# Seven products instead of eight for the last three query projections of an attention kernel, with their operand sums kept in spare parts of other tiles

## The chip, the cores and the metric

The kernel runs on one core of one Trainium2 chip. Its time is the device time of one execution in microseconds (us), given as the median of several runs.

The engines go by these names: TensorE (PE in the profile; PEld is its weight load), VectorE (DVE), ScalarE (ACT), GpSimd (POOL) and SyncE (SP, which issues most of the DMAs here). Each works through its own queue in order and waits on semaphores for the others.

## The reference

Everything is fp32: one sequence of 1,024 rows, 512 wide. Causal attention has 32 query heads on 8 key and value heads, 128 wide. It sits between two layer norms and a residual, and a feed-forward layer with a routed low-rank part follows. Cut to what matters:

```python
n = layernorm(x)                                   # (1024, 512)
q = (n @ w_q).reshape(S, 8, 4, 128)                # 8 groups of 4 query heads
k = (n @ w_k).reshape(S, 8, 128)
v = (n @ w_v).reshape(S, 8, 128)
scores = einsum("qhgd,khd->hgqk", q, k) * 128 ** -0.5
probs = softmax(where(causal, scores, -inf))
attn = einsum("hgqk,khd->qhgd", probs, v).reshape(S, 4096) @ w_o
x = x + layernorm(attn)
h = layernorm(x)
y = h @ base_W.T + base_b + lora(h, softmax router over 15 logits)
out = x + layernorm(y)
```

## The kernel before, in words

**Blocks and pairs.** A block is one key/value group g (0 to 7, with its four query heads) and one tile t of 128 query rows: 64 blocks, `blocks[i]`, in the order in which they run. Two neighbouring blocks, tiles 2u and 2u + 1 of one group, make a pair; `pairs[m]` holds blocks 2m and 2m + 1. The first 24 pairs go through groups 0 to 5. The last eight (from block N2 = 48 on) take the groups 6 and 7 in turn, with u in the order 0, 3, 2, 1. So the last blocks are:

| pair m | blocks i | group, tiles | key columns up to |
|---|---|---|---|
| 26, 27 | 52-53, 54-55 | 6 and 7, tiles 6 and 7 | 1024 |
| 28, 29 | 56-57, 58-59 | 6 and 7, tiles 4 and 5 | 768 |
| 30, 31 | 60-61, 62-63 | 6 and 7, tiles 2 and 3 | 512 |

**A block.** The loop over i computes a block's scores in four parts (`scores(g, t, j)`, four times 32 rows for four heads). Each part is one or two matmuls into PSUM, then on VectorE the mask (L622) and the row maximum (L624), on ScalarE the exponential (L629) and, after a reciprocal (L636), the scaling (L637), and on VectorE a transpose into the tile T (L643). The scaling and the transpose of a part are issued inside the next part's call, those of the last part inside the next block's first. GpSimd writes zeros to the end of the row (`memset`, L627). After the fourth part 16 DMAs on SyncE's queue copy T, rearranged, into the tile K (`to_keys`). T and K are "block-row tiles": one of each for even tiles t and one for odd ones (`turn_tile`), of 3,584 and 4,096 words per partition, of which a block fills (t + 1) x 512.

**What fills TensorE between the parts.** Between the score parts stand pieces of other work, cut into four shares by their number of columns (`run_share`):
- `pv`: the value products (`po`) of the block two before, one piece of 512 columns for each key tile;
- `o`: the output projection (`pO`) of block i - 3 where that belongs to group 7, after which a row is complete and its norm steps follow; `o_pair` is the same for a pair of the other groups;
- `begins` and `ends`: the router and the feed-forward layer of a finished row;
- `q`: the query projection of the next pair, in the odd blocks. It must be done when the next block's first scores start.

Steps of the norms and of the router on VectorE and GpSimd are put in a list (`defer`) and taken from it one or more at each score part (`work_off`).

**Two forms of the query projection.** `project_q` multiplies directly: 16 matmuls of 256 columns, two PSUM banks, two ScalarE copies (L429). `project_q_halves` splits weights and tokens into two by two quarters and forms the product from seven products of sums instead of eight products of quarters: 28 matmuls of 128 columns, four PSUM banks taken from a pool of three, one ScalarE copy (L480), and six VectorE additions (`add`, L454) that merge the products into the query tile qT. It needs sums of the weight quarters (`combine_w`, L145, four GpSimd operations for each load of a group's weights) and of the token quarters (`combine_x`, L188, four more for each u). Pairs in `QW`, which are 2 to 27, use this form; pairs 0, 1 and 28 to 31 use the direct one.

**What sets the order.** `keep` and `order` pin an instruction behind everything already written for its engine; VectorE's additions at L454 and ScalarE's copies of queries are not pinned. The tile framework adds the waits. The tiles `wq` have one buffer: the next group's weights (`load_q`, SyncE, at the start of an even block) wait for the last product that reads the old ones.

Of the kernel before, what the change touches and what calls it, by code (L numbers as in the profile page):

```python
# [9 lines left out]
F32 = mybir.dt.float32  # L10
I32 = mybir.dt.int32
AF = mybir.ActivationFunctionType
ALU = mybir.AluOpType
AX = mybir.AxisListType

P = 128
# [6 lines left out]
def kernel(  # L23
# [33 lines left out]
    nc = tc.nc  # L57
# [4 lines left out]
    NT = S // P  # L62
    KC = H // P
    QB = 512
    NQB = S // QB
    TPB = QB // P
    PQ = 2 * P
    SQ = P // R
    NSUB = P // SQ
# [11 lines left out]
    turn = ctx.enter_context(tc.tile_pool(name="turn", bufs=1))  # L81
# [6 lines left out]
    pairs = [(g, u) for g in range(G - 2) for u in range(NT // 2)]  # L88
    pairs += [(g, u) for u in (0, 3, 2, 1) for g in (G - 2, G - 1)]
    blocks = [(g, 2 * u + e) for g, u in pairs for e in range(2)]  # L90
    N = len(blocks)
    N2 = (G - 2) * NT
    QW = range(2, N2 // 2 + 4)

    def keep(ins):
        return tc.keep_in_program_order(ins)
# [5 lines left out]
    def matmul(*args, **kw):  # L102
        keep(nc.tensor.matmul(*args, **kw))  # L103
# [6 lines left out]

    def turn_tile(kind, g, t):

        size = (NT - 1 + t % 2) * NSUB * P
        return turn.tile([P, size], F32, tag=f"{kind}{t % 2}", name=f"{kind}_{g}_{t}")

    weights = {}

# [119 lines left out]
    xnT = [big.tile([P, KC, QB], F32, tag=f"xnT{b}", name=f"xnT_{b}") for b in range(NQB)]  # L237
# [72 lines left out]
    def bank(name):  # L310
        return ps_m.tile([P, 512], F32, tag="pm", name=name)
# [104 lines left out]
    def project_q(g, u):  # L416

        pm = {}

        def get(j):  # L420
            if j % 2 == 0:
                pm[0] = bank(f"pq_{g}_{u}_{j}")
            return pm[0][:, ts(j % 2, PQ)]

        def finish(j):
            if j == 0:
                qTs[g, u] = act.tile([P, PQ // SQ, R, SQ], F32, tag="qT", name=f"qT_{g}_{u}")
            if j % 2:
                nc.scalar.copy(  # L429
                    qTs[g, u][:, :, j - 1 : j + 1, :].rearrange("p s h q -> p h s q"),  # L430
                    pm[0].rearrange("p (h s q) -> p h s q", h=2, q=SQ),
                )

        def term(j, c):
            w = weights["q", j // 2]
            assert w[0] == g
            rhs = xnT[u * PQ // QB][:, c, ts(u % (QB // PQ), PQ)]
            return w[1][:, c, ts(j % 2, D)], rhs

        work = []  # L440
        for j in range(R):
            terms = [lambda j=j, c=c: term(j, c) for c in range(KC)]
            if j == 0:
                ends = lambda pm: finish(0)
            else:
                ends = lambda pm, j=j: finish(j)
            work += chained(lambda j=j: get(j), terms, ends, PQ)
        return work
# [4 lines left out]
    def add(dst, src, to):  # L453
        nc.vector.tensor_tensor(dst, src, to, ALU.add)  # L454

    def project_q_halves(m):


        g, u = pairs[m]
        hk = KC // 2  # L460
        pm = {}

        def half(e, h):

            return both(e)[:, h]

        def both(e):
            q = qTs[g, u][:, ts(e, NSUB), :, :]
            return q.rearrange("p s (x h) q -> p x s (h q)", x=2)

        def each(x):

            return qTs[g, u].rearrange("p s (x h) q -> p x s (h q)", x=2)[:, x]

        def merge(b):

            one, two = pm[b][:, 0], pm[b][:, 1]
            if b == 0:
                q = each(0).rearrange("p (e s) n -> p e s n", e=2)
                nc.scalar.copy(q, one.unsqueeze(1).to_broadcast([P, 2, NSUB, 2 * SQ]))  # L480
                add(half(0, 0), two, half(0, 0))
            elif b == 1:
                add(half(1, 0), one, half(1, 0))
                add(half(1, 1), two, half(1, 0))
            elif b == 2:
                add(half(0, 1), one, half(1, 1))
                add(half(1, 0), two, half(1, 0))
            else:
                add(both(1), one.unsqueeze(1).to_broadcast([P, 2, NSUB, 2 * SQ]), both(1))

        def piece(n, c, k):
            i, b, x = PRODUCTS[n], n // 2, n % 2
            if n == c == k == 0:
                qTs[g, u] = act.tile([P, PQ // SQ, R, SQ], F32, tag="qT", name=f"qT_{g}_{u}")
            if x == c == k == 0:
                whole = bank(f"pq_{g}_{u}_{b}")
                pm[b] = whole.rearrange("p (x s n) -> p x s n", x=2, s=NSUB)
            assert weights["sq"] == (g,) and weights["tx of"] == u
            matmul(
                pm[b][:, x, :, ts(c, SQ)],  # L500
                weights["sq", 0][i][:, k, ts(c, D)],
                weights["tx"][i][:, k, :].rearrange("p (s q) -> p s q", q=SQ),
                start=(k == 0),
                stop=(k == hk - 1),
            )
            if c == 1 and k == hk - 1 and (x == 1 or n == 6):
                merge(b)

        return [
            (P, lambda n=n, c=c, k=k: piece(n, c, k))  # L510
            for n in range(7)
            for c in range(2)
            for k in range(hk)
        ]
# [50 lines left out]
        return project_halves(f"v{gv}", u, ("sv", gv), lambda w, x: (x, w), quarters)  # L565

    turned, keyed = {}, {}

    def turn_view(w, t):
        n = t + 1  # L570
        return w[:, : n * NSUB * P].rearrange("p (b s k q) -> p b s k q", b=R, s=NSUB, k=n)
# [29 lines left out]
    def rescale_scores():  # L601
        if "rescale" in score_tile:
            score_tile.pop("rescale")()
# [325 lines left out]
    c, d, e, f = (blocks[k][1] for k in (N - 6, N - 5, N - 2, N - 1))  # L929
    later = {}  # L930

    def projections(i):
# [10 lines left out]
        elif i % 2 and m < len(pairs) and i not in (N2 + 1, N2 + 5):  # L943
            q = project_q_halves(m) if m in QW else project_q(*pairs[m])
        first = GV
# [114 lines left out]
    def attend(i):  # L1060
        return weighted_values(*blocks[i])

    ready = []
    for i in range(N):
        loads(i)
        q, other = projections(i)
        pv = attend(i - 2) if i >= 2 else []
        o, o_pair, ends, begins = [], [], [], []
        for t in complete(i, 3):
            o = project_o(*blocks[i - 3])  # L1070
        if i % 2 == 0 and i >= 4 and blocks[i - 4][0] < G - 1:
            if i == 4:
                rescale_scores()
            o_pair = project_o_pair(*pairs[i // 2 - 2])
        for t in complete(i, 6, 7):
            ends = sum(ffn_out(t), [])
        for t in complete(i, 5):
            begins = ffn_router(t)

        rest = o + weave(o_pair, other + pv[:2] + begins[1:] + pv[2:])  # L1080
        if i in (N2, N2 + NT // 2):
            rest = weave(o_pair, pv) + other
        if i == N2 + 1:
            rest = pv[:3] + other + pv[3:]

        if i % 2 and i // 2 + 1 in QW and blocks[i][1] > 1 and i > 3:
            cut = len(rest) * 3 // 5
            q, rest = weave(q, rest[:cut]), rest[cut:]
        then = begins[:1] + q + ends[:-1] + rest[:4] + ends[-1:] + rest[4:]
        shares = [n / NSUB for n in range(NSUB + 1)]  # L1090
        if o_pair and blocks[i][0] % 2 == 0 and blocks[i][1] == 2 and i < N2:

            shares[3] = 0.8
        for n in range(NSUB):
            scores(*blocks[i], n)
            run_share(then, shares[n], shares[n + 1])
            m = i // 2 + 1
            if i % 2 == 0 and m in QW:
                if n == 0 and i < N2:
                    combine_x(pairs[m][1], m)  # L1100
                if n == (1 if i < N2 else 0):
                    combine_q(m)
            g, t = blocks[i]
            if g % 2 and g + 1 < G and n == 1:
                if t == 6:
                    combine_k(g + 1)
                if t == 7:
                    combine_v((g + 1) // GV)
            if (i, n) in ((N2, 3), (N2 + 1, 2), (N2 + 2, 2)):
                combine_x(i - N2 + 1, 0)  # L1110
        if i == 1:
            combine_o(0)
        if i == NT:
            prepare_ffn()
        if i == NT + 4:
            prepare_map()
        for t in complete(i, 2):
            reload_x(t)
        ready += complete(i, 7, 8)
        for t in [t for t in ready if ("done", t) in state]:  # L1120
            ready.remove(t)
            ffn_store(t)

        if i >= NT and blocks[i - 2][1] == 0 and blocks[i - 2][0] < G - 1:
            combine_o(blocks[i - 2][0])
# [79 lines left out]
```

## Time and profile before

| what | value |
|---|---|
| median of 3 runs | 1059.7 us (1059.08 to 1059.84) |
| the profiled execution, its own time | 1059.33 us |
| its span, first to last instruction | 1057.3 us |
| TensorE busy | 1043.3 us, 99% |
| VectorE busy | 748.2 us, 71% |
| ScalarE busy | 477.9 us, 45% |
| GpSimd busy | 267.5 us, 25% |
| mean granted TensorE clock | 0.998 |

The last blocks begin, by TensorE's timeline, at 869.30 (block 56), 891.46 (57), 913.50 (58), 929.96 (59), 948.27 (60), 966.69 (61), 985.30 (62) and 997.97 us (63). What follows 1006 us is the end of the last rows' feed-forward layer.

How to read the lines: in the timeline a line begins with the start in us from the span's beginning and the busy time of the merged instructions; then engine, source line, operation, output <- inputs by the program's names, their shapes, and xN, the number of records. An fp32 matmul is two records. A bracket gives the idle time of the engine just before, and what ended it. In the answer on waits a line is: who waited, for whom, us in total, times, and the longest.

### The profile page before, as it was taken

How to read it: one execution, taken by the hardware profiler on the slowest of the kernel's cores; microseconds unless marked ns; L12 is line 12 of the kernel's file. 1: busy time of each engine (PE TensorE's matmuls, PEld its weight loads, DVE VectorE, ACT ScalarE, POOL GpSimd, SP SyncE). 2: the span in 40 equal slices, each digit the busy share in tenths (PEclk: the TensorE clock that was granted, in tenths of full speed). 3: DMA queues.
4: the chain of work that ended last, by engine and by line, in shares of the span. 5: the costliest groups of instructions: out<-in, count | busy, mean ns of one | idle time of the engine just before them, and what ended most of it. 6: DMA issues, size and time to landing. Idle time of an engine off the chain costs nothing.

```text
span 1057.3 us, 15637 instructions
## 1 busy us (share of the span) xinstructions
PE 1043.3 (99%) x4864; PEld 732.0 (69%) x4864; DVE 748.2 (71%) x1831; ACT 477.9 (45%) x962; POOL 267.5 (25%) x502
## 2 busy tenths in 40 slices
PE   8999999999999999999999999999999999999996
PEld 7766677767787676767787667767888466566453
DVE  4576657876687766887487866886667966576666
ACT  2655435553244544554244544654234654454421
POOL 2613125241131214241130312442162110111212
PEclk9999999999999999999999999999999999999999
DMA  5145352563125452453324452464333674543331
GB/s 189 32 125 138 77 122 70 146 152 87 33 54 160 95 118 63 120 150 82 73 51 122 108 113 66 131 168 112 87 108 87 166 173 104 140 106 99 81 91 40
DMA packets 78513, 111.99 MB, mean 106 GB/s; under 512 B 18176, under 2 KB 49920, under 8 KB 78432
## 3 DMA queue, kind: packets, MB, share of 16 engines
q1 hardware_dynamic: 74960, 105.71, 39.8%
q0 software_dynamic: 2096, 3.46, 1.4%
q10 hardware_dynamic: 1376, 1.84, 0.5%
q8 instruction: 39, 0.64, 0.3%
q14 instruction: 42, 0.34, 0.1%
HBM read 33.34 MB, written 2.10 MB: 34 GB/s over the span
## 4 chain that ended last, share of the span: by engine, by line
PE 92%; DVE 3%; SPq 2%; ACT 1%; DMA 1%; issue 1%; POOL 0%; POOLq 0%; ACTq 0%; DVEq 0%
PE po L103 22%; PE s L103 21%; PE pq L103 19%; PE pv L103 5%; PE pe L103 4%; PE pk L103 4%; PE pa L103 4%; PE pf L103 3%; PE pO L103 3%; PE pc L103 2%; PE pb L103 2%; PE pd L103 2%; SPq L109 2%; PE pl L103 1%; DVE nmax L624 1%
## 5 line engine op out<-in xcount | busy, mean ns | idle before, releaser
L637 ACT ACTIVATE p<-p,rec 128x32 f32<-128x32 f32 (+31 forms) x256 | 188.1, 735 | 233.7 <-DVE rec L636 177.1
L103 PE MATMUL po<-K,v 128*128 128x512 f32 x576 | 280.5, 594 | 0.7 <-DMA wo<-in_w_o_dram 0.6
L103 PE MATMUL s<-kT,qT 128*128 128x512 f32 (+15 forms) x768 | 272.4, 464 | 0.8 <-ACT p L629 0.7
L629 ACT ACTIVATE p<-s,nmax 128x32 f32<-128x32 f32 (+31 forms) x256 | 179.3, 700 | 165.5 <-DVE nmax L624 151.0
L643 DVE STREAM_TRANSPOSE T<-p 128x128 f32<-128x128 f32 (+7 forms) x256 | 197.6, 774 | 54.2 <-ACT p L637 42.8
L103 PEld LDWEIGHTS s<-kT,qT 128*128 128x128 f32 x768 | 140.5, 190 | 117.0 <-issue 105.2
L624 DVE TENSOR_REDUCE nmax<-s 128x1 f32<-128x32 f32 (+31 forms) x256 | 180.1, 703 | 7.2
L103 PEld LDWEIGHTS po<-K,v 128*128 128x128 f32 x576 | 103.5, 190 | 59.9 <-issue 50.6
L627 POOL MEMSET p<- 128x96 f32 (+2 forms) x192 | 29.1, 156 | 420.3 <-DVE T L643 387.0
L622 DVE TENSOR_TENSOR s<-s,smask 128x32 f32<-128x32 f32 x256 | 47.8, 187 | 86.4 <-PE s L103 85.6
L103 PE MATMUL pq<-xnT,wq 128*128 128x128 f32 (+1 forms) x608 | 97.5, 308 | 0.0
L454 DVE TENSOR_TENSOR qT<-pq,qT 128x256 f32<-128x256 f32 x156 | 70.0, 460 | 35.9 <-ACT qT L480 19.6
L103 PEld LDWEIGHTS pq<-xnT,wq 128*128 128x128 f32 x608 | 87.5, 191 | 11.3 <-issue 6.6
L188 POOL TENSOR_TENSOR tx<-xnT 128x256 f32<-128x256 f32 x52 | 37.8, 727 | 183.4 <-PE pv L103 95.3
L674 ACT COPY attnT<-po 128x512 f32<-128x512 f32 x64 | 37.3, 583 | 74.0 <-PE po L103 73.7
L103 PE MATMUL pa<-wo,attnT 128*128 128x256 f32 x224 | 58.5, 385 | 0.0
L103 PEld LDWEIGHTS pq<-tx,wq 128*128 128x128 f32 x416 | 53.0, 192 | 7.9 <-issue 7.5
L103 PE MATMUL pq<-tx,sq 128*128 128x128 f32 x416 | 57.5, 275 | 0.0
L103 PEld LDWEIGHTS pq<-tx,sq 128*128 128x128 f32 x416 | 53.4, 192 | 5.7 <-issue 5.0
L103 PE MATMUL pq<-tx,wq 128*128 128x128 f32 x416 | 55.4, 275 | 0.0
L103 PEld LDWEIGHTS pa<-wo,attnT 128*128 128x128 f32 x224 | 41.1, 190 | 14.1 <-issue 9.3
L636 DVE RECIPROCAL rec<-total 128x1 f32<-128x1 f32 x256 | 39.2, 153 | 15.7 <-ACT p L629 14.5
(152 smaller groups left out, 1286.2 us busy)
## 6 DMA issues: line engine op xcount, KB each, us to landing
K<-T SPq DMA_DIRECT2D x128, 128.0 KB, 2.4
K<-T SPq DMA_DIRECT2D x128, 112.0 KB, 2.3
wq<-in_w_q_dram SPq DMA_DIRECT2D x27, 512.0 KB, 5.0
K<-T SPq DMA_DIRECT2D x128, 96.0 KB, 2.2
K<-T SPq DMA_DIRECT2D x128, 80.0 KB, 2.1
wo<-in_w_o_dram SPq DMA_DIRECT2D x32, 256.0 KB, 3.9
K<-T SPq DMA_DIRECT2D x108, 64.0 KB, 2.0
K<-T SPq DMA_DIRECT2D x113, 48.0 KB, 2.0
```

The costliest lines, as they stand in the source:

```text
L103: keep(nc.tensor.matmul(*args, **kw))
L109: keep(by.dma_start(dst, src))
L188: nc.gpsimd.tensor_tensor(dst, p, q, ALU.subtract)
L454: nc.vector.tensor_tensor(dst, src, to, ALU.add)
L622: keep(nc.vector.tensor_tensor(s[:, n - SQ : n], s[:, n - SQ : n], smask, ALU.add))
L624: keep(nc.vector.tensor_reduce(nmax, s[:, :n], AX.X, ALU.max, negate=True))
L627: nc.gpsimd.memset(p[:, n:full], 0.0)
L629: keep(nc.scalar.activation(p[:, :n], s[:, :n], AF.Exp, bias=nmax, accum_out=total))
L636: keep(nc.vector.reciprocal(rec, total))
L637: keep(nc.scalar.mul(p[:, :n], p[:, :n], rec))
L643: nc.vector.transpose(turned[g, t][:, :, j, :, :].rearrange("p b k q -> p k b q"), p[:, :full].rearrange("p (k b q) -> p k b q", b=R, q=SQ),)
L674: copy = nc.scalar.copy(o, po)
```

## The change

Pairs 29, 30 and 31 (the new list `QL`) go over to the seven-product form. Pair 28 stays direct.

Their sums get no tiles of their own. Blocks 54 and 55 (group 7, tiles 6 and 7) are the last that fill T and K to the end. From them on `turn_tile` returns the same four tiles again (`long_tiles`) instead of new ones. The following blocks fill at most six of their eight parts (five of seven in the even ones), and `spare` gives out the parts behind: three for the weight sums s1, s2, s4 (two in the even T, one in the odd T) and two for the four token sums t1 to t4 (in the even K). The fourth weight sum replaces the quarter a21 in place, as before.

The sums are written as a list (`last_sums`) when part 2 of the even block before is issued, and pinned on GpSimd in portions (`LATE`): two after part 2 and two after part 3 of the even block, the remaining four (the token sums, for pairs 29 and 30) after part 0 of the odd block. Pair 31 uses the token sums of pair 30.

In the odd blocks 57, 59 and 61 the query pieces move: they stood at the head of the block's pieces and now stand before the last four (`rest[cut:]`), and what stood behind them (pO, the value products, the router's products) comes earlier.

```diff
-    QW = range(2, N2 // 2 + 4)
+    QL = range(N2 // 2 + 5, N // 2)
+    QW = [*range(2, N2 // 2 + 4), *QL]
...
     def turn_tile(kind, g, t):
 
+        if (kind, t % 2) in long_tiles:
+            return long_tiles[kind, t % 2]
         size = (NT - 1 + t % 2) * NSUB * P
-        return turn.tile([P, size], F32, tag=f"{kind}{t % 2}", name=f"{kind}_{g}_{t}")
+        w = turn.tile([P, size], F32, tag=f"{kind}{t % 2}", name=f"{kind}_{g}_{t}")
+        if (g, t) in blocks[N2 + 6 : N2 + 8]:
+            long_tiles[kind, t % 2] = w
+        return w
+
+    def spare(kind, e, n):
+
+        at = (NT - 3 + e + n) * NSUB * P
+        return long_tiles[kind, e][:, at : at + NSUB * P].rearrange("p (k n) -> p k n", k=KC // 2)
+
+    def last_sums(m):
+
+        g, u = pairs[m]
+        w = [weights["q", i][1] for i in range(2)]
+        hk = KC // 2
+        a11, a12, a21, a22 = w[0][:, :hk], w[0][:, hk:], w[1][:, :hk], w[1][:, hk:]
+        s1, s2, s4 = spare("T", 0, 0), spare("T", 0, 1), spare("T", 1, 0)
+        xp = xnT[u * PQ // QB][:, :, ts(u % (QB // PQ), PQ)]
+        b11, b12, b21, b22 = xp[:, :hk, :P], xp[:, :hk, P:], xp[:, hk:, :P], xp[:, hk:, P:]
+        t1, t2, t3, t4 = (spare("K", 0, n // 2)[:, :, ts(n % 2, P)] for n in range(4))
+        todo = [
+            (s1, a21, a22, ALU.add),
+            (s2, s1, a11, ALU.subtract),
+            (a21, a11, a21, ALU.subtract),
+            (s4, a12, s2, ALU.subtract),
+        ]
+        if weights["tx of"] != u or m == QL[0]:
+            todo += [
+                (t1, b12, b11, ALU.subtract),
+                (t2, b22, t1, ALU.subtract),
+                (t3, b22, b12, ALU.subtract),
+                (t4, b21, t2, ALU.subtract),
+            ]
+        weights["sq", 0] = (a11, a12, s4, a22, s1, s2, a21)
+        weights["sq"] = (g,)
+        weights["tx"] = (b11, b21, b22, t4, t1, t2, t3)
+        weights["tx of"] = u
+        return todo
+
+    long_tiles = {}
+
+    LATE = {(e, n): k for e, ks in enumerate(((0, 0, 2, 2), (4, 0, 0, 0))) for n, k in enumerate(ks)}
...
-        if i % 2 and i // 2 + 1 in QW and blocks[i][1] > 1 and i > 3:
+        if i % 2 and i // 2 + 1 in QW and blocks[i][1] > 1 and 3 < i < N2:
             cut = len(rest) * 3 // 5
             q, rest = weave(q, rest[:cut]), rest[cut:]
         then = begins[:1] + q + ends[:-1] + rest[:4] + ends[-1:] + rest[4:]
+        if i % 2 and i // 2 + 1 in QL:
+            cut = max(4, len(rest) - 4)
+            then = begins[:1] + ends[:-1] + rest[:4] + ends[-1:] + rest[4:cut] + q + rest[cut:]
...
             scores(*blocks[i], n)
             run_share(then, shares[n], shares[n + 1])
             m = i // 2 + 1
-            if i % 2 == 0 and m in QW:
+            if i % 2 == 0 and m in QL and n == 2:
+                todo.extend(last_sums(m))
+            if i >= N2 + NT and i // 2 + 1 in QL:
+                for dst, p, q, op in [todo.pop(0) for _ in range(min(LATE[i % 2, n], len(todo)))]:
+                    keep(nc.gpsimd.tensor_tensor(dst, p, q, op))
+            if i % 2 == 0 and m in QW and m not in QL:
```

The bound `3 < i < N2` leaves the weaving of earlier blocks as it was. At block 53, where the old condition held too, there are no query pieces and no router or feed-forward pieces, so that the order there is the same.

More of the change, by code (lines that the diff above doesn't have):

```diff
@@ L492, in piece @@
             i, b, x = PRODUCTS[n], n // 2, n % 2
+            assert not todo
             if n == c == k == 0:
@@ L567 @@
     turned, keyed = {}, {}
+    todo = []
     def turn_view(w, t):
```

## The prediction

> **What bounds the kernel now.** I read the page's totals and its chain first, then TensorE's waits, then its timeline where the edited work stands, then VectorE's timeline at the same places.
>
> ```profile
> span 1057.3 us, 15637 instructions
> ...
> PE 1043.3 (99%) x4864; PEld 732.0 (69%) x4864; DVE 748.2 (71%) x1831; ACT 477.9 (45%) x962; POOL 267.5 (25%) x502
> ...
> PE 92%; DVE 3%; SPq 2%; ACT 1%; DMA 1%; issue 1%; POOL 0%; POOLq 0%; ACTq 0%; DVEq 0%
> ```
>
> TensorE (PE) is busy 99% of the span and is 92% of the chain that ended last. VectorE has 29% of the span idle and GpSimd 75%. All that TensorE waited for, in the whole span, is this:
>
> ```profile
> PE idle L106 <- POOL ident masks.py:199: 1.5, 1, 1.5
> ...
> PE s L103 <- ACT p L629: 0.7, 2, 0.3
> PE pc L103 <- DVE acc L748: 0.7, 1, 0.7
> PE po L103 <- DMA wo<-in_w_o_dram: 0.6, 1, 0.6
> ...
> PE pd L103 <- DVE hw L836: 0.3, 1, 0.3
> ```
>
> No wait in this answer, small ones included, is as long as 2 us. So TensorE's instruction stream is the time, and two things count: how long the stream becomes, and whether a new wait appears in it. Its length has to be read as pitch, start to start, because the durations overlap. These are seven-product queries of pair 26, the form that the last three pairs get, and then the ordinary queries of pair 30, one of the three:
>
> ```profile
> 815.88 1.67 PE L103 MATMUL s<-kT,qT 128*128 128x512 f32 x4
> 817.39 1.72 PE L103 MATMUL pq<-tx,wq 128*128 128x128 f32 x14
> 818.95 1.06 PE L103 MATMUL pq<-xnT,sq 128*128 128x128 f32 x8
> 819.84 1.06 PE L103 MATMUL pq<-tx,sq 128*128 128x128 f32 x8
> 820.73 1.72 PE L103 MATMUL s<-kT,qT 128*128 128x512 f32 x4
> ```
>
> ```profile
> 931.53 3.19 PE L103 MATMUL pq<-xnT,wq 128*128 128x256 f32 x14
> 934.55 1.35 PE L103 MATMUL s<-kT,qT 128*128 128x512 f32 x4
> 935.73 3.19 PE L103 MATMUL pq<-xnT,wq 128*128 128x256 f32 x14
> 938.76 1.40 PE L103 MATMUL s<-kT,qT 128*128 128x512 f32 x4
> 939.99 1.03 PE L103 MATMUL pq<-xnT,wq 128*128 128x256 f32 x4
> ```
>
> Each fp32 matmul is two records. From 817.39 to 820.73 there are 30 records of 128 columns: 3.34/30 = 0.111 us each. From 931.53 to 934.55 there are 14 of 256 columns: 0.216 us each; 935.73 to 938.76 gives the same. A 512-column matmul (two records) takes 0.858 us in the same timeline.
>
> **The change, part by part.** *TensorE, removed and added.* An ordinary pair is 16 matmuls, 32 records x 0.2162 = 6.92 us. A seven-product pair is 28 matmuls, 56 records x 0.1113 = 6.23 us. Three pairs: 3 x 0.69 = **2.05 us saved**. This is 0.19% of the run, so even the whole of it stays just inside the 0.2% that a measurement of this kernel can tell from no change.
>
> [...]
>
> *ScalarE and VectorE.* A pair loses one of its two 0.585 us ScalarE copies and gains five adds of 128x256 (0.42 us) and one of 128x512 (0.69): 2.8 us of VectorE. In the windows of the three blocks that compute queries (57, 59, 61) VectorE is busy 11.3 of 22.0, 12.2 of 18.3 and 9.8 of 18.6 us. It fits; only the time of the last add matters (below).
>
> *GpSimd.* Three weight groups of four 128x512 sums (1.27 us each in the trace) and two token groups of four 128x256 (0.73): 15.2 + 5.8 = 21 us on an engine that is a quarter busy. The orders that count: the sums of group 29 run after scores 2 and 3 of block 56 and the token sums after scores 0 of block 57 (897 to 900 behind the waiting `acc` addition of 895.85), and the first product that needs them starts at 903.7. In block 59 the token sums stand behind `rstd_h` (934.2) and end at about 937.4, t2 at 936.0; product 3 needs it at 937.4 and product 4 needs t3 at 938.3. Queued behind these sums are pad memsets and the next `rstd` powers; both have microseconds until a transpose or a norm needs them. Cost on the path 0; if the cover went, each 0.73 us sum late would stop TensorE for as long.
>
> *SyncE.* No DMA is added. The next load of `wq` waits for the last product that reads the old one (the twentieth of 28 pieces): 906.3 in block 57, 941.3 in block 59, while SyncE reaches that load at 907.43 and 944.28. So the copies of T to K queued behind it are not held.
>
> *What moves.* In blocks 57, 59 and 61 the products go from the front to just before the last pieces of PV. I laid the pieces on the pitches, a block's four quarters being cut by columns; times are those of the shortened stream:
> - Block 57: four pO and one po, scores, three po and 6 products, scores, 19 products, scores, 3 products (end 909.4), four po (3.43 us); block 58's scores at 912.85 (913.50 now).
> - Block 59: turn, two po, router products, one po, scores, 12 products, scores, 14, scores, 2 (end 944.36), three po (2.57 us); block 60's scores at 946.93.
> - Block 61: 17 products before the last scores, 1 after (end 979.8), four po; block 62's scores at 983.25.
>
> PV of block 57's K now starts at 930.9 instead of 940.9; the last of the 16 copies of that K is issued at 926.1 and lands 2.1 us later, at 928.2. pO in block 57 starts at 892.6; its `attnT` copy is done at 892.25. Block 59's router products start at 932.6, hT's copy ends by 931.7. All three fit, the second by only 0.3 us. The products take four PSUM banks in turn from a pool of three, where ordinary queries took two: in block 59 the third (940.4) reuses the router's `pl`, free when `hw` is made at about 939.9; a late route there would stop TensorE by its lateness.
>
> *The new wait.* The last add (128x512) writes half of the whole query tile, so the next block's first scores wait for it. It stands on VectorE behind the last scores' work of the block. For seven-product queries and for block 59 the trace has these rows:
>
> ```profile
> 818.83 1.10 DVE L643 STREAM_TRANSPOSE T<-p 128x896 f32<-128x896 f32 x1
> 819.85 2.50 DVE L454 TENSOR_TENSOR qT<-pq,qT 128x256 f32<-128x256 f32 x5
> ```
>
> ```profile
> 945.28 0.96 DVE L624 TENSOR_REDUCE nmax<-s 128x1 f32<-128x768 f32 x1
> 946.15 0.97 DVE L643 STREAM_TRANSPOSE T<-p 128x768 f32<-128x768 f32 x1
> ```
>
> The first pair shows that adds queue behind the row maximum and the transpose: products ended at 820.73, the adds at 822.35. With block 59's new order: last scores end at 943.91, mask and maximum (0.96) to 945.3, transpose (0.97) to 946.2, then the row's next deferred step, which is y's statistics (0.65 + 0.18 + 0.15) because the router moved ahead, to 947.2, then the add to 947.9, some 948.0 with the hand-over, against 946.93 when TensorE gets there: up to 1.1 us of waiting. The add is not pinned and can slip in front of the statistics: then 947.0, a wait of 0.1. By the same sum block 57's add ends at 912.8 against 912.85, and block 61's at 983.0 against 983.25. Bounds: 0 (all adds early, or the four free `rest` pieces cover them) and, if five adds come as one run of 2.50 us behind the statistics, 1.8 + 2.9 + 1.5 = 6.2 us. I take 0.8 us: block 59's sum mostly in force, the other two met.
>
> Sum: -2.05 + 0.8 = **-1.25 us**. Made on the profiled execution: span 1057.3 to about 1056.05, with the 2.03 us around it (its own time is 1059.33) 1058.1. That execution is 0.37 us under the median of the runs, 1059.7, so the median becomes **1058.5**.
>
> **The rivals.** *The adds come late in all three pairs (slower).* One mechanism: VectorE runs its queue in order, and the five adds of a pair bunch as they did at 819.85, after the last scores' maximum, transpose and statistics. Place: first scores of blocks 58, 60, 62. Price: 6.2 us in full, net +4.15, 1063.9. It decides as soon as the three waits add up to more than 2.05 us, and is beyond 0.2% above 4.2 us. For it: the run of five at 819.85. Against: in the new order 24 or more of the 28 products lie before the last scores, so four of the adds can run in VectorE's idle stretch before them (2.90 us of idle before the scores of 909.41). More likely in part than in full.
>
> *No wait at all.* All adds slip in and block 61's earlier pO takes its norm steps out of blocks 62 and 63, where VectorE is busy 9.3 of 12.7 and 7.0 of 8.0 us; the tail's single wait of 0.29 us could go too. -2.05 to -2.4: 1057.3 to 1057.65. Against: block 59's margin is negative by my sum.
>
> *The sums are not free of the tile they lie in.* If waits were kept per tile, not per part, the token sums of block 57 would wait for the copies of K of block 56 (last landing about 908, needed at 903.7) and those of block 59 for block 58's (about 946, needed at 937): 5 + 11 us of stall, net about +14, 1074. The trace speaks against it, on a tile of the same kind, the input rows held in a K tile:
>
> ```profile
> 4.54 0.69 DVE L331 BATCH_NORM_STATS2 stats_x<-K_x 128x6 f32<-128x512 f32 x1 [4.54 <-DMA K_x<-in_x_dram]
> ...
> 13.57 0.69 DVE L331 BATCH_NORM_STATS2 stats_x<-K_x 128x6 f32<-128x512 f32 x1 [1.38 <-DMA K_x<-in_x_dram]
> ```
>
> Row 0 is read at 4.54 while another row of the same tile makes VectorE wait for its DMA until 13.57: parts are waited for separately.
>
> **How the numbers follow.** My forecast, waits of 0.1 to 1.6 us in sum, 1057.7 to 1059.2: 0.62. No wait or a small gain more: 0.14, of which about 0.10 lie beyond 0.2% below (under 1057.6). Late adds: 0.18, split between within 0.2% (0.09) and beyond (0.09). Tile-wide waits, or sums late on GpSimd: 0.06, all slower. Faster 0.10, same 0.71, slower 0.19. The range takes the forecast, the no-wait case and the late adds up to waits of 3.5 us: 1057.3 to 1061.2.
>
> **What would show it.** Right: `pq` records of 256 columns in blocks 57, 59 and 61 replaced by 56 of 128 at 0.111 us; scores of block 58 beginning about 0.65 us earlier than 913.50; a single TensorE wait on VectorE's `qT` of 0.3 to 1.1 us at about 947; GpSimd 21 us busier; no wait on GpSimd or on a DMA of K. Wrong: waits on `qT` at all three block starts (late adds), TensorE waiting for the sums on GpSimd or GpSimd waiting for SyncE's copies (tile), a pitch well over 0.111 us with the sums as weights.

## The result, and the profile after

The changed kernel takes **1057.63 us** in the median of 12 runs (1056.39 to 1058.32), against 1059.61 us for 12 runs of the kernel before: ratio 0.9978, 95% interval 0.9971 to 0.9985. In a second set of runs it was 1057.57 against 1059.89 us, ratio 0.9979 (0.9970 to 0.9988). So it is faster by about 2 us, 0.2%, which is nearly all that the shorter stream offers; 1058.5 was predicted.

The page of the changed kernel: its span, the busy line and the chain by engine.

```profile
span 1056.3 us, 15824 instructions
...
PE 1041.1 (99%) x4936; PEld 732.1 (69%) x4936; DVE 757.2 (72%) x1849; ACT 477.0 (45%) x959; POOL 288.0 (27%) x522
...
PE 92%; DVE 3%; SPq 2%; ACT 1%; DMA 1%; issue 1%; POOL 0%; POOLq 0%; DVEq 0%; ACTq 0%
```

TensorE is still 99% busy and 92% of the chain. GpSimd has 20.5 us more than before (288.0 against 267.5) and VectorE 9.0 more; neither shows in the chain. Three lines of the answer on TensorE's waits (who waited, for whom: us in total, times, longest):

```profile
PE ptx_x L109 <- DVE K_x L390: 1.2, 1, 1.2
PE s L106 <- DVE qT L500: 0.9, 1, 0.9
...
PE po L106 <- DMA K<-T: 0.2, 1, 0.2
```

The only wait for a query tile, 0.9 us, lies at 57.45 us, at the first scores of block 4, where both kernels issue the same instructions. It is not one of the three that the prediction spoke of, but it shows what such scores wait for. VectorE there in the changed kernel, then TensorE:

```profile
56.92 0.72 DVE L500 TENSOR_TENSOR qT<-pq,qT 128x256 f32<-128x256 f32 x2
...
59.74 0.67 DVE L500 TENSOR_TENSOR qT<-pq,qT 128x512 f32<-128x512 f32 x1
```

```profile
57.45 1.24 PE L106 MATMUL s<-kT,qT 128*128 128x512 f32 x4 [0.85 <-DVE qT L500]
```

The two additions at 56.92 belong to the third of the four PSUM banks. The first of them writes the half of the query tile that the even block reads and ends at 57.31 (0.39 us); the scores start 0.14 us later, and 2.3 us before the last addition (128x512, at 59.74) begins. The kernel before has the same place, VectorE and then TensorE:

```profile
56.15 0.72 DVE L454 TENSOR_TENSOR qT<-pq,qT 128x256 f32<-128x256 f32 x2
...
58.98 0.68 DVE L454 TENSOR_TENSOR qT<-pq,qT 128x512 f32<-128x512 f32 x1
```

```profile
56.68 1.24 PE L103 MATMUL s<-kT,qT 128*128 128x512 f32 x4
```

In both profiles block 4's first scores start 0.53 us after the third bank's additions begin (56.15 and 56.68, 56.92 and 57.45), whether TensorE's line shows idle time before them (0.85 us) or none, and 2.3 us before the last addition begins. So the profile before already held the answer to the question on which the prediction turned: do the even block's scores wait for the last addition?

The wait for `K<-T` (0.2 us) is new and small; the experiment e8 below takes it up.

The span fell by only 1.0 us (1057.3 to 1056.3), less than the medians, and that can be placed. Block 57 begins at 892.49 here and began at 891.46 before, though TensorE's order of instructions is identical up to there. Some 0.7 us of this arises at block 4: the value products before its first scores start at 54.66 and 54.71, the scores at 56.68 and 57.45. In the nine profiles of the changed kernel and its variants block 57's start lies anywhere from 891.05 to 892.49. From block 57 on the comparison is sharp. The length of each block is the difference between the starts of its own and the next block's first `s` records in TensorE's timeline:

| profile | 57 | 58 | 59 | 60 | 61 | 62 | 63 to the end | 57 to the end |
|---|---|---|---|---|---|---|---|---|
| before | 22.04 | 16.46 | 18.31 | 18.42 | 18.61 | 12.67 | 59.33 | 165.84 |
| after | 21.39 | 16.46 | 17.66 | 18.41 | 17.95 | 12.68 | 59.26 | 163.81 |
| e0_changed | 21.39 | 16.46 | 17.66 | 18.42 | 17.95 | 12.67 | 59.28 | 163.83 |
| e1_order_only | 22.05 | 16.46 | 18.31 | 18.42 | 18.60 | 12.68 | 59.27 | 165.79 |
| e2_products_first | 31.04 | 16.46 | 21.94 | 18.43 | 17.94 | 12.68 | 59.16 | 177.65 |
| e3_gate_even_half | 21.40 | 16.45 | 18.63 | 18.50 | 17.95 | 12.67 | 59.25 | 164.85 |
| e4_products_last | 21.39 | 16.54 | 18.85 | 18.49 | 17.95 | 12.67 | 59.61 | 165.50 |
| e5_sums_once | 21.39 | 16.45 | 17.67 | 18.41 | 17.95 | 12.67 | 59.31 | 163.85 |
| e7_two_pairs | 22.05 | 16.45 | 17.66 | 18.42 | 17.95 | 12.67 | 59.24 | 164.44 |
| e8_split_copies | 21.39 | 16.45 | 17.67 | 18.42 | 17.95 | 12.67 | 59.34 | 163.89 |

Blocks 57, 59 and 61, which compute the queries, are 0.65, 0.65 and 0.66 us shorter; no other block changed by more than 0.01. The sum is 1.96 us, and 2.03 to the end. Between two profiles an unchanged block agrees to 0.02 us, so that these rows tell much more than the medians, whose runs spread over 1 to 2 us.

The place that should have held the wait, in the changed kernel. First TensorE's timeline of block 59 up to block 60's first scores:

```profile
936.64 1.95 PE L106 MATMUL pq<-xnT,wq 128*128 128x128 f32 x16
938.43 1.06 PE L106 MATMUL pq<-K,T 128*128 128x128 f32 x8
939.32 1.40 PE L106 MATMUL s<-kT,qT 128*128 128x512 f32 x4
940.56 1.95 PE L106 MATMUL pq<-K,wq 128*128 128x128 f32 x16
942.34 1.06 PE L106 MATMUL pq<-xnT,T 128*128 128x128 f32 x8
943.24 0.61 PE L106 MATMUL pq<-K,T 128*128 128x128 f32 x4
943.68 1.46 PE L106 MATMUL s<-kT,qT 128*128 128x512 f32 x4
944.98 0.61 PE L106 MATMUL pq<-K,T 128*128 128x128 f32 x4
945.42 2.74 PE L106 MATMUL po<-K,v 128*128 128x512 f32 x6
948.00 0.65 PE L106 MATMUL s<-kT,qT 128*128 128x288 f32 x2
```

The 56 `pq` records lie where the prediction laid them: 12 matmuls, scores, 14, scores, 2. The sources K and T are the spare parts with the sums. From 936.64 to 939.32 there are 24 records at 0.112 us. Then three value products (six `po` records) and, at 948.00 with no idle time, block 60's first scores. VectorE at the same time:

```profile
943.40 1.73 DVE L500 TENSOR_TENSOR qT<-pq,qT 128x256 f32<-128x256 f32 x4
...
946.29 0.97 DVE L691 STREAM_TRANSPOSE T<-p 128x768 f32<-128x768 f32 x1
947.18 0.65 DVE L334 BATCH_NORM_STATS2 stats_y<-y 128x6 f32<-128x512 f32 x1
947.75 0.67 DVE L500 TENSOR_TENSOR qT<-pq,qT 128x512 f32<-128x512 f32 x1
948.34 0.17 DVE L336 BATCH_NORM_AGGREGATE mv_y<-stats_y 128x2 f32<-128x6 f32 x1
```

The last addition (128x512) starts at 947.75, behind the transpose and half of y's statistics, and VectorE's next instruction starts at 948.34; by its own duration the addition ends at 948.42. Counted from block 59's start (930.34 here, 929.28 in the prediction's schedule) the addition ends after 18.0 us, where I had summed 18.6, and the scores begin after 17.66 us, where I had 17.65. So the addition is indeed late, by 0.34 us at least. But the scores began before it had ended: they did not wait for it. At blocks 58 and 62 the last addition ends before TensorE gets there (913.22 against 913.88, 981.82 against 984.36), so these two places say nothing about the wait.

### The profile page after: what moved, and what is told of

It reads as the page before. It is cut to its first block, busy times and chain, and to the rows that moved or that the text cites. A ratio compares the mean times of both kernels' runs of the same rounds, so it can differ in the third digit from the quotient of the medians.

```text
span 1056.3 us, 15824 instructions
## 1 busy us (share of the span) xinstructions
PE 1041.1 (99%) x4936; PEld 732.1 (69%) x4936; DVE 757.2 (72%) x1849; ACT 477.0 (45%) x959; POOL 288.0 (27%) x522
## 4 chain that ended last, share of the span: by engine, by line
PE 92%; DVE 3%; SPq 2%; ACT 1%; DMA 1%; issue 1%; POOL 0%; POOLq 0%; DVEq 0%; ACTq 0%
PE po L106 22%; PE s L106 21%; PE pq L106 18%; PE pv L106 5%; PE pe L106 4%; PE pk L106 4%; PE pa L106 4%; PE pf L106 3%; PE pO L106 3%; PE pc L106 2%; PE pb L106 2%; PE pd L106 2%; SPq L112 2%; PE pl L106 1%; DVE nmax L672 1%
## 5 line engine op out<-in xcount | busy, mean ns | idle before, releaser
L685 ACT ACTIVATE p<-p,rec 128x32 f32<-128x32 f32 (+31 forms) x256 | 188.1, 735 | 240.9 <-DVE rec L684 184.0
L500 DVE TENSOR_TENSOR qT<-pq,qT 128x256 f32<-128x256 f32 x174 | 77.9, 461 | 38.2 <-ACT qT L526 21.1
L106 PEld LDWEIGHTS pq<-xnT,wq 128*128 128x128 f32 x560 | 75.4, 191 | 9.5 <-issue 6.6
L106 PE MATMUL pq<-xnT,wq 128*128 128x128 f32 (+1 forms) x560 | 81.6, 293 | 0.0
```

What stands on the lines that cost most here:

```text
L685: keep(nc.scalar.mul(p[:, :n], p[:, :n], rec))
```

## The experiments

The competing theories. **A**: the last addition writes only the half of the query tile that the pair's odd block reads; the even block, which comes next, needs only the additions before it, and the shorter stream comes through whole. **B**: the prediction, in which the last addition is waited for. **C**: the gain comes from the moved order, not from the products. Every run has its block lengths in the table above; they tell the theories apart better than the medians do.

**e0_changed**: the changed kernel beside the others, with no edit.

> The changed kernel itself, beside the others on one chip. Theory A (the last addition writes only the odd half of the query tile, so that the next block's first scores do not wait for it, and the shorter stream comes through whole): 2.0 us under the kernel before. Theory B (the prediction: the last addition is waited for, about 0.8 us of the 2.05 is lost): 1.2 us under it. Theory C (the gain comes from the moved order, not from the products): also 2.0 us under it.

1057.57 us, ratio 0.9979 (0.9970 to 0.9988), 2.3 us under the kernel before, and the same block lengths as in the first profile. Against B's 1.2 us; A and C stand.

**e1_order_only**:

```diff
-            q = project_q_halves(m) if m in QW else project_q(*pairs[m])
+            q = project_q_halves(m) if m in QW and m not in QL else project_q(*pairs[m])
...
-            if i % 2 == 0 and m in QL and n == 2:
+            if False and m in QL and n == 2:
```

> The queries of pairs 29 to 31 in the direct form (32 records of 256 columns), but at the late place of the change; no sums on GpSimd. Theory A: the stream is as long as before, 1059.6, within 0.4 us. Theory C: about 2 us under the kernel before, as the change. Theory B says the same as A here, since the two ScalarE copies of the direct form take 0.6 us and 2.6 to 3.4 us of value products stand behind them.

1059.34 us against 1059.89, ratio 0.9997 (0.9988 to 1.0005); blocks 57, 59 and 61 are 22.05, 18.31 and 18.60 us, as before the change. The moved order by itself gains nothing, C falls.

**e7_two_pairs**:

```diff
-    QL = range(N2 // 2 + 5, N // 2)
+    QL = range(N2 // 2 + 6, N // 2)
```

> Only pairs 30 and 31 in the seven-product form and at the late place; pair 29 direct and at the head, as before. Theory A: two thirds of the gain, 1.35 us under the kernel before, in the trace 0.65 to 0.69 us less in blocks 59 and 61 and nothing in block 57. Theory C or a fixed gain at one place: 0 or 2.0 us under it.

1058.41 us against 1059.54, ratio 0.9989 (0.9980 to 0.9998). The table shows the dose: block 57 back at 22.05, blocks 59 and 61 at 17.66 and 17.95. Each pair brings its own 0.65 us.

**e3_gate_even_half**: the wait that the prediction supposed, made real by a multiplication by 1.0 behind the last addition, on the half that it does not write.

```diff
                 add(both(1), one.unsqueeze(1).to_broadcast([P, 2, NSUB, 2 * SQ]), both(1))
+                if m in QL:
+                    keep(nc.vector.tensor_scalar(both(0), both(0), 1.0, None, ALU.mult))
```

> The change plus, for pairs 29 to 31, a VectorE multiplication of the even half of the query tile by 1.0 (about 0.55 us) pinned behind the last addition: now the next block's first scores do wait for work behind the last addition, the wait that the prediction supposed. Theory A: block 60's first scores wait about 0.9 us (the addition ends at 948.3 in the changed kernel's trace, plus 0.55 and the hand-over, against TensorE at 948.0), block 58's 0 to 0.1, block 62's none; 0.9 us over the changed kernel. Theory B (the scores wait for the last addition already): 0.5 us or less over the changed kernel, and the trace of the changed kernel should have shown a wait of its own.

1058.89 us against 1059.89 before, ratio 0.9991 (0.9982 to 1.0000), 1.3 us over e0_changed by the medians and 1.0 by the blocks. TensorE in this run:

```profile
945.39 2.74 PE L106 MATMUL po<-K,v 128*128 128x512 f32 x6
948.93 0.72 PE L106 MATMUL s<-kT,qT 128*128 128x288 f32 x2 [0.81 <-DVE ve_y L338]
```

and VectorE:

```profile
947.72 0.67 DVE L500 TENSOR_TENSOR qT<-pq,qT 128x512 f32<-128x512 f32 x1
948.31 0.17 DVE L336 BATCH_NORM_AGGREGATE mv_y<-stats_y 128x2 f32<-128x6 f32 x1
948.39 0.40 DVE L537 TENSOR_SCALAR qT<-qT 128x512 f32<-128x512 f32 x1
948.70 0.15 DVE L338 TENSOR_SCALAR ve_y<-mv_y 128x1 f32<-128x1 f32 x1
```

The multiplication starts at 948.39, took 0.40 us where I had put 0.55, and block 60's scores start at 948.93, 0.14 us after it ends, with the first instruction behind it named as the releaser. The bracket gives 0.81 us of idle time, and block 59 is 0.97 us longer than in e0_changed: in an unbroken stream neighbouring TensorE lines overlap by 0.16 us (945.42 + 2.74 against 948.00 above), which the bracket doesn't count. Blocks 57 and 61 are unchanged to 0.01 us.

So work behind the last addition holds the scores, at the place that the prediction named, if that work writes the even half. In the changed kernel none does. The size is not a confirmation of the predicted 0.8 us, since the multiplication itself is 0.40 us of it: had the scores waited for the last addition alone (end 948.42, and 0.14 us more), an estimate from these numbers is a start at 948.56, 0.56 us late.

**e4_products_last**: no value products between the seven products and the next block.

```diff
-            cut = max(4, len(rest) - 4)
+            cut = len(rest)
```

> The seven products at the very end of blocks 57, 59 and 61, with no value products between them and the next block's scores. Theory A: the scores wait for the additions of the third bank, which stand behind the last scores' maximum, transpose and statistics: about 0.6 us in block 58, 1.7 in block 60, 0.5 in block 62, 2.8 in sum, so 0.75 us over the kernel before (1060.4). Theory B (for the last addition too): another 0.5 to 0.7 us each, about 2.8 us over it.

1058.75 us against 1059.54, ratio 0.9994 (0.9985 to 1.0003): 165.50 us from block 57 to the end against 163.83 for the change, so slower than that, but faster than either theory had put it. The waits were 0, 1.02 and 0 us at blocks 58, 60 and 62 where I had summed 0.6, 1.7 and 0.5; a further 0.9 us wait on the value products of block 63 left the end 0.35 us later. Block 60 in this run, TensorE and then VectorE:

```profile
947.00 1.06 PE L106 MATMUL pq<-K,T 128*128 128x128 f32 x8
949.08 0.72 PE L106 MATMUL s<-kT,qT 128*128 128x288 f32 x2 [1.02 <-ACT p L685]
```

```profile
948.51 1.55 DVE L500 TENSOR_TENSOR qT<-pq,qT 128x256 f32<-128x256 f32 x3
949.98 0.19 DVE L670 TENSOR_TENSOR s<-s,smask 128x32 f32<-128x32 f32 x1
```

The run of three at 948.51 is the third bank's two additions and the last one. The scores start at 949.08. The first of the three, about 0.42 us long, is over at about 948.93; all three are over only near 950.0. Of the third bank's additions the first writes the even half, `half(0, 1)`; the second writes the odd half, as the last does. The scores start some 0.15 us after the first, as at block 4. The bracket names another releaser, ScalarE's scaling of `p` (L685), but the scores don't read `p`, and in e3_gate_even_half VectorE's transpose waits for the same scaling until 951.59, long after block 60's first scores at 948.93. A holds and B falls. Of the 0.7 us by which I overpriced block 60, the third bank's second addition, which I had counted too, is some 0.4 us; the rest, and the missing waits of blocks 58 and 62, were not taken apart.

**e5_sums_once**:

```diff
-        return todo
+        return todo if m == QL[0] else []
```

> The change with the sums computed for pair 29 alone; pairs 30 and 31 multiply with sums left from it, so that 12 GpSimd operations (8 of 128x512 or 4 of them, and 4 of 128x256: 13 us of GpSimd) are left out and the queries of those two pairs are other numbers. Theory A: GpSimd's sums are hidden, the same as the changed kernel within 0.3 us. If they slow VectorE or hold up its norm steps on the path: 0.5 us or more under the changed kernel.

1057.19 us against 1059.54, ratio 0.9979 (0.9971 to 0.9988), and 163.85 us from block 57 to the end against 163.83: leaving the sums of two pairs out gains nothing. At the late place these additions of GpSimd are hidden, and they slow no other engine on the path.

**e2_products_first**: seven products at the old place.

```diff
-        if i % 2 and i // 2 + 1 in QL:
+        if False:
             cut = max(4, len(rest) - 4)
...
-    LATE = ... ((0, 0, 2, 2), (4, 0, 0, 0)) ...
+    LATE = ... ((0, 0, 2, 6), (0, 0, 0, 0)) ...
```

> Seven products at the head of blocks 57, 59 and 61, where the direct form stood; the token sums are issued after part 3 of the even block, so that they precede them. If the late place only gives GpSimd time (theory A): in block 59 the sum t2 ends at about 936.4 behind the residual addition and two weight sums, while TensorE needs it at about 933.7, so TensorE waits some 2.5 us for GpSimd there, none in blocks 57 and 61, and the run is 0.4 us over the kernel before (1060.0). If the late place has no use: 2.0 us under it, as the change. Theory B: the additions have the whole block to finish, so 2.05 us under it.

1069.34 us against 1059.89, ratio 1.0084 (1.0070 to 1.0098): 9.5 us slower than the kernel before, where I had expected 0.4. Two things were missing in my sum. The first is a wait in block 57. TensorE and GpSimd there:

```profile
892.58 1.95 PE L106 MATMUL pq<-xnT,wq 128*128 128x128 f32 x16
901.00 2.08 PE L106 MATMUL pq<-K,T 128*128 128x128 f32 x8 [6.48 <-POOL K L1153]
902.88 3.19 PE L106 MATMUL pq<-K,wq 128*128 128x128 f32 x14
```

```profile
895.50 0.12 POOL L675 MEMSET p<- 128x32 f32 x1 [5.41 <-DVE T L691]
896.99 1.26 POOL L922 TENSOR_TENSOR acc<-y,acc 128x512 f32<-128x512 f32 x1 [1.36 <-ACT y L350]
898.21 1.26 POOL L1153 TENSOR_TENSOR T<-wq,T 128x512 f32<-128x512 f32 x1
899.42 0.72 POOL L1153 TENSOR_TENSOR K<-xnT 128x256 f32<-128x256 f32 x1
900.23 0.72 POOL L1153 TENSOR_TENSOR K<-xnT,K 128x256 f32<-128x256 f32 x1
```

Three weight sums were done by 889.9. Then GpSimd's queue held two other instructions in front of the fourth and the token sums, though these were written first in the program: a `memset` of the tile `p`, which sat 5.41 us until VectorE had transposed what was in that buffer, and y's residual addition (`acc`, 896.99), which sat 1.36 us for ScalarE's norm of y. So the sums ran from 898.2 on, and TensorE stood 6.48 us until the second token sum (900.23) was there. In block 59 the wait was 2.61 us, as expected (2.5); in block 61, whose sums were in time, there was none, and the block took 17.94 us at the old place as at the late one. An order of GpSimd's queue with the sums in front was not tried. The second is what the two waits of this run cost afterwards. Windows of the same run (length, then busy time and count for each engine, the granted TensorE clock, DMA share and GB/s):

```profile
core 0: us, PE busy (x) PEld busy (x) DVE busy (x) ACT busy (x) POOL busy (x), PEclk, DMA share, GB/s
885.00:894.50 9.50, 9.50 (x43) 6.43 (x41) 8.27 (x23) 3.44 (x7) 4.49 (x6) 1.00 0.18 45
894.50:901.00 6.50, 0.03 (x1) 0.00 (x0) 1.47 (x4) 2.17 (x5) 4.06 (x6) 0.68 0.38 88
901.00:904.00 3.00, 3.00 (x14) 3.00 (x15) 0.00 (x0) 0.00 (x0) 1.32 (x2) 0.50 0.60 140
904.00:907.00 3.00, 3.00 (x12) 2.48 (x12) 0.92 (x3) 0.86 (x1) 0.00 (x0) 0.50 0.45 102
907.00:911.00 4.00, 4.00 (x25) 3.01 (x25) 3.00 (x6) 0.94 (x2) 0.00 (x0) 0.99 0.84 229
```

The clock column reads 1.00 until the wait, and 0.50 for six microseconds after it: the eight records at 901.00 took 2.08 us, where eight take 1.06 us in the changed kernel. Block 57 is 9.65 us longer than in e0_changed, 6.48 of it wait and nearly all of the rest half speed; block 59 is 4.28 us longer for a wait of 2.61.

**e8_split_copies**: a possible better version, for the new wait of 0.2 to 0.4 us on the copies of block 61's K.

```diff
-                alone = not short and at < N - 1
+                alone = not short and at < N - 1 and at != N - 3
```

> The change, and of the 16 copies of K of block 61 five go by GpSimd's queue, eleven by SyncE's. The changed kernel waits 0.2 to 0.4 us in block 63 for the last of these copies, which the kernel before did not. If SyncE's issue rate (16 copies in 10 us) is what is late: that wait is gone, 0.3 us under the changed kernel, about 2.3 us under the kernel before, too little to tell in the medians but plain in the trace. If GpSimd's copies land later than SyncE's last one, or hold up its norm steps: the wait stays or grows.

1057.44 us against 1059.43, ratio 0.9983 (0.9974 to 0.9992). The wait is gone from TensorE's answer, and nothing is gained: 59.34 us from block 63 to the end against 59.28. The end of the last rows takes 59.2 to 59.3 us from block 63 in every profile where block 63 itself isn't held longer; which of its chains absorbs the 0.3 us is not shown. None of the variants beats the change.

## Why the prediction was wrong, point by point

- **What bounds the kernel** held. The gain is the shortening of TensorE's stream in the three blocks; the moved order adds nothing (e1, e7).
- **TensorE's saving**, 2.05 us from the pitches: 1.96 in the three blocks. The pitch of the 128-column records came out at 0.112 us instead of 0.1113. It is measured from start to start, so that whatever the weight loads cost is in it: PEld was busy 732.1 us with 4936 loads, against 732.0 us with 4864 before.
- **The new wait** is the step that failed. It said: "The last add (128x512) writes half of the whole query tile, so the next block's first scores wait for it." The first clause is true and the second doesn't follow. The half is `both(1)`, the odd block's rows, needed a whole block later. I priced the time at which the addition would end without asking who reads what it writes. Its 0.8 us measured 0, and -1.25 us became -1.96 to -2.03. The time itself was also 0.6 us off, since the addition came between the steps of y's statistics and not behind them; so even a real wait would have been about 0.56 us. e3 makes the scores wait at that place by writing the even half last. Block 4 of the profile before, where the same form of the query projection runs and the scores start 2.3 us ahead of the last addition, would have shown the mistake.
- **The late-adds rival**, priced at up to 6.2 us, rested on the same misreading. Its bunch of additions is real (four in a run at 943.40), but only those on the even half can hold the next block. With at least 24 of the 28 products before the last scores, their products come early enough: in block 59 the whole run of four is over at 945.1, and TensorE gets to block 60 at 948.00. e4 shows how far one has to go to make them late: to the end of the block, for 1.02 us in one block of three.
- **The no-wait case** was worked out as 1057.3 to 1057.65 and given 0.14. Its number is what happened, its reason is not: "All adds slip in" is false for block 59, where the last addition did come late and nothing waited for it. Its argument against itself, that "block 59's margin is negative", was right about the margin and wrong about its effect. The part of it that spoke of a further gain in the tail cannot be told from 0: 59.26 against 59.33 us.
- **The tile-wide waits** did not come. GpSimd, then SyncE, in the changed kernel:

```profile
897.53 1.27 POOL L922 TENSOR_TENSOR acc<-y,acc 128x512 f32<-128x512 f32 x1 [0.87 <-ACT y L350]
898.75 0.73 POOL L1153 TENSOR_TENSOR K<-xnT 128x256 f32<-128x256 f32 x1
899.57 0.73 POOL L1153 TENSOR_TENSOR K<-xnT,K 128x256 f32<-128x256 f32 x1
...
901.62 1.27 POOL L1153 TENSOR_TENSOR T<-wq,T 128x512 f32<-128x512 f32 x1
```

```profile
896.54 10.82 SPq L112 DMA_DIRECT2D K<-T  x16
```

The token sums go into K from 898.75 on, while SyncE issues the 16 copies of block 56 into other parts of that K from 896.54 to 907.4.
- **GpSimd's cover** held at 0: nothing waits for a sum in the changed kernel, and leaving 12 of them out gains nothing (e5). One weight sum of pair 29 (`T<-wq,T`) did not come after part 3 of block 56 but at 901.62, behind the token sums that were written after it, so pinning did not keep its place; the record does not show why. Its product starts at 907.37. The sentence on its price, that a late sum "would stop TensorE for as long", put the price too low: in e2 6.48 us of wait cost 9.65, and 2.61 cost 4.28.
- **SyncE and PSUM** held: no wait on `wq`, on the router's `pl` or on a bank appears in the changed kernel.
- **The shares.** By the prediction's own pieces "same" adds up to 0.62 + 0.04 + 0.09 = 0.75 and "slower" to 0.09 + 0.06 = 0.15, where it wrote 0.71 and 0.19.

## What to carry to other kernels

When an instruction moves close to a consumer, write down which part of the buffer it writes and which part the consumer reads before pricing the time at which it ends; in a kernel that keeps dependences by part, the last writer of a tile is often not what the next reader waits for. Before laying out a schedule for a form that the kernel already uses elsewhere, look in the profile for a place where it runs: here the consumer's start beside the last addition, at block 4, answers the question in three lines. When a tightly packed engine is the bound, compare stretches that both kernels share (here block by block, to 0.02 us) instead of spans, whose first part can drift by more than the effect. A later place for work that needs operands from a slower queue can still be what makes a change pay: e1 shows that it gains nothing by itself, and e2 that without it, in that order of GpSimd's queue, the same products lose 9.5 us.

## What the runs showed of the hardware that was not expected

In e2_products_first two stalls of TensorE cost more than their length: against e0_changed block 57 grew by 9.65 us for a wait of 6.48, block 59 by 4.28 for one of 2.61. After the 6.48 us the granted clock was 0.50 from 901 to 907 us and 0.99 from 907 to 911. After the 2.61 us it was 0.50 in the window from 945 to 947 us, 0.74 from 947 to 949 and 1.00 from 949 to 951. After the short waits of e3 and e4 (0.81 and 1.02 us) the window from 948 to 952 us shows 1.00 in both.

The windows in which the mean clock changes place the edges, if it is 1.00 on one side and 0.50 on the other; these are estimates from those means. The clock fell at about 896.84 (0.68 from 894.5 to 901.0) and 944.64 (0.94 from 942.0 to 945.0), 2.3 and 2.2 us after the end of the last matmul. It rose at about 907.08 (0.99 from 907.0 to 911.0) and 948.04 (0.74 from 947.0 to 949.0), 6.1 and 3.0 us after the start of the next one. The wait, half of the time that TensorE then ran at half speed and the overlap of 0.16 us add up to 9.7 and 4.3 us, against 9.65 and 4.28 measured. Two cases do not show what sets these delays.
